# Graph attention, then self-attention: second batch's self_feat as seven half products, gathered additions one a slot, background work moved

## The chip, the cores and the metric

The kernel runs on one core of a Trainium2 chip. The metric is device time in microseconds (us) for one execution. A core has several engines, each working through its own queue in order: TensorE (PE; matmuls and transposes), VectorE (DVE), ScalarE (ACT), GpSimd (POOL) and SyncE (SP), which issues DMAs. An engine waits for another's result through semaphores. A queue is strictly in order: an instruction that waits holds up everything behind it on its engine.

## The reference, cut to what matters

Two layers run over x of shape (8, 512, 512), float32. The change touches layer 0 only.

```
def layer0(v, q, adj, ...):                    # B=8, N=512, F=512, 16 heads, 20 neighbours
    row_zero = v.sum(-1) == 0
    q_exp = where(row_zero[..., None], 0, q[:, None, :])
    self_feat = concat([v, q_exp], -1) @ W_self.T + b_self
    output = self_feat
    for d in range(2):
        A = adj or its transpose, [:, :, :20, :]
        cond, vb = A.sum(-1), A @ w_bias + b_bias
        output += gat_attention(self_feat, cond, vb, Wq[d], bq[d], Wk[d], bk[d], Wout[d], bout[d])
    return v + relu(output)

def gat_attention(self_feat, cond, vb, ...):
    kv = self_feat[:, :20]
    aff = (q . k) / sqrt(dh);  aff = where(cond > 0, aff, -9e15) + vb
    w = softmax(aff)                           # over the 20 neighbours
    return (w @ kv) through Wout, per head
```

Layer 1 is a conditional layer norm, a 16-head self-attention with softmax, an output projection, a residual and a second conditional layer norm.

## The kernel before

**Layout.** P = 128 partitions, so a batch of 512 rows is C = 4 row blocks. B = 8 batches times 4 blocks gives 32 *slots* (b, c), numbered n = 4b + c. Layer 0 walks through the slots; layer 1 follows with 16 steps a batch. The instruction order is written out by hand (`manual_schedule`), so the order of the source is the order of each engine's queue.

**One slot of layer 0, as the main loop writes it.** `turn_weights(n)` transposes the finished softmax weights of slot n on PE (`ptw`, L564) and ACT copies them (L566). `normalize0(n+1)`: exponential on ACT (L553), sum `den` (L556) and reciprocal (L557) on DVE, multiplication on POOL (L558). `scores0(n+2)`: 8 matmuls `pss` (L532) on PE, two additions of the query row on DVE (L536), the mask multiplication on POOL (L538). `add_edges(n+2)`: POOL (L542). Then come products for a later batch's self_feat. `result0(n)`: matmuls `po` (L574, L576) on PE, x = relu + x on DVE (L577), a store. `edges` for a later batch (DVE, L258 to L264), between whose halves `less_top(n+2)` stands: maximum `top` on DVE (L549), subtraction on POOL (L550). Then come loads and background work at the end of the slot. So slot n+2's weights pass L536, L538, L542, L549 and L550 in slot n, and L553, L556, L557 and L558 in slot n+1.

A PE matmul of float32 appears in the profile as two rows, so "x8" of L359 is one product of four matmuls, and "x8" of L312 is four matmuls of 512 columns.

**self_feat in seven products.** For batches 2 to 7, W_self and the transposed x are split in quarters, and the eight quarter products are replaced by seven (numbered 1 to 7, in `self_feat_product`, L359), with sums of weight quarters (`weight_sums0`, L338, DVE, once) and of x quarters (`turned_sums`, L345, POOL, four a batch). Products 1, 6 and 7 build up running sums `ys` (L364 on ACT, L369 on DVE) and add to the list TO_ADD0 one, one and two pending additions of such a sum onto a quarter of self_feat. These are the gathered additions (L699, DVE). Products 2 to 5 are added directly (L373). In slots with c = 2 and 3 products (1, 2) and (6, 7) of batch b + 2 are made, in slots with c = 0 and 1 products (4, 5) and (3) of batch b + 1. At the end of each slot, all pending additions run: one after c = 2, three after c = 3. Batches 0 and 1 use the plain form, 16 matmuls of 512 columns (L312) and an addition for each of four blocks (L320).

**Other background work.** `live_sums(b+2)` (ACT, four sums over rows of x, L293, and one small DVE instruction `lt`, L295) stands at the end of slots with c = 0; `live_of(b+2)` (four PE transposes `pl`, L301, ACT copy, L303) before `result0` in slots with c = 1. `far_away(b+1)` (DVE, L269, L270) stands at the end of slots with c = 1. `norm_stats` (DVE L93 to L96, POOL L97) of layer 1's first batch stand at the end of slots 15 to 18, `norm` (L111) at the end of 22 and 23, two each. In slots 24 and 25 `turn` (L124, PE) transposes what `norm` made.

**PSUM.** Single banks come in turn from a pool of four (products, `po`, `pl`, `pw`), pairs of banks from a pool of two (`pss`, `ptw`).

Of the kernel before, what the change touches and what calls it, by code (L numbers as in the profile page):

```python
# [9 lines left out]
F32 = mybir.dt.float32  # L10
# [3 lines left out]
ALU = mybir.AluOpType  # L14
# [4 lines left out]
B, N, F = 8, 512, 512  # L19
P = 128  # L20
# [5 lines left out]
D2 = 2 * NG  # L26
# [18 lines left out]
def graph_then_self_attention(ctx: ExitStack, tc: tile.TileContext, x, x_t, near, near_t, labels, w_self_t, wq, wk_t,  # L45
# [128 lines left out]
    with ExitStack() as l0:  # L174
# [40 lines left out]
        def load_vt(b):  # L215
            VT[b] = turned.tile([P, C, N], F32, tag="turned", name=f"vt_{b}")
            for cut in (slice(0, 2), slice(2, C)) if b == 0 else (slice(0, C),):
                nc.sync.dma_start(VT[b][:, cut], blocks(x_t[b])[:, cut])
# [20 lines left out]
            nc.vector.memset(head[DH * j:DH * (j + 1), j:j + 1], 1.0)  # L239

        MASK, ADD, LABELS = {}, {}, {}

        def load_labels(b, halves=(0, 1)):
            for i in halves:
                LABELS[b, i] = two.tile([P, 2, D2 * L], I32, tag="labels", name=f"labels_{b}_{i}")
                nc.sync.dma_start(LABELS[b, i], labels[b, i * N // 2:(i + 1) * N // 2, :].rearrange("(c p) m -> p c m", p=P))

        def edges(b, c, halves=(0, 1)):


            if c == 0 and 0 in halves:
                MASK[b] = two.tile([P, C, D2], F32, tag="mask", name=f"mask_{b}")
                ADD[b] = two.tile([P, C, D2], F32, tag="add", name=f"add_{b}")
            src = LABELS[b, c // 2][:, c % 2, :].rearrange("p (m l) -> p m l", l=L)
            weighted = src.bitcast(F32)
            total = two.tile([P, D2], F32, tag="total", name=f"total_{b}_{c}_{halves[0]}")
            if 0 in halves:
                nc.vector.tensor_reduce(total, src, AX.X, ALU.add)  # L258
                nc.vector.tensor_scalar(MASK[b][:, c, :], total, 0.0, None, ALU.is_gt)
            if 1 not in halves:  # L260
                return
            nc.vector.tensor_tensor(weighted, src, edge_bc[:, None, 0:L].to_broadcast([P, D2, L]), ALU.mult)
            nc.vector.tensor_reduce(total, weighted, AX.X, ALU.add)
            nc.vector.tensor_scalar(ADD[b][:, c, :], total, edge_bc[:, L:L + 1], None, ALU.add)  # L264

        def far_away(b):

# [29 lines left out]
        def live_of(b):  # L297

            pl = bank(f"pl_{b}") if b else pair("pl_0")[:, 0, :]
            for c in range(C):  # L300
                nc.tensor.transpose(pl[:, c * P:(c + 1) * P], LT[b][:, c:c + 1].to_broadcast([P, P]), ident)  # L301
            LIVE[b] = two.tile([P, N], F32, tag="live", name=f"live_{b}")
            nc.scalar.copy(LIVE[b], pl)  # L303
# [18 lines left out]
        def self_feat(b, blocks_of_f):  # L322

            self_feat_rest(b, self_feat_main(b, blocks_of_f))
# [15 lines left out]
        def turned_sums(b, n):  # L340

            B11, B12, B21, B22 = (quarter(VT[b], p, q) for p in range(2) for q in range(2))
            TB[n] = {0: B12, 3: B21}.get(n) or parts.tile([P, 2, M], F32, tag=f"t{n}", name=f"ts{n + 1}_{b}")
            x0, x1 = ((B12, B11), (B22, TB.get(0)), (B22, B12), (B21, TB.get(1)))[n]
            nc.gpsimd.tensor_tensor(TB[n], x0, x1, ALU.subtract)  # L345

        def self_feat_product(b, n):
# [24 lines left out]
            for p, q in {2: ((0, 0),), 3: ((0, 1),), 4: ((1, 0),), 5: ((1, 1), (0, 1))}.get(n, ()):  # L372
                nc.vector.tensor_tensor(quarter(SF[b], p, q), o, quarter(SF[b], p, q), ALU.add)  # L373

        def q_row(b):
            QR[b] = two.tile([P, HM], F32, tag="q_row", name=f"q_row_{b}")
            nc.sync.dma_start(QR[b], q_d[b].partition_broadcast(P))
# [54 lines left out]
        far_away(0)  # L432
        load_vt(1)
        load_labels(1)

        kt = pro.tile([P, 2, HG, 2 * MH], F32, name="kt")
        made = kv.tile([P, C, HM], F32, tag="kv", name="made").rearrange("p c m -> p (c m)")
# [103 lines left out]
        def add_edges(b, c, engine=nc.gpsimd):  # L541
            engine.tensor_tensor(T[b, c], T[b, c], ADD[b][:, c, None].to_broadcast([P, H, D2]), ALU.add)  # L542
# [26 lines left out]
        def result0(b, c):  # L569
            cut = slice(c * P, (c + 1) * P)  # L570
            po = bank(f"po_{b}_{c}")

            for g in range(HG):
                nc.tensor.matmul(po[:, g * P:(g + 1) * P], SF[b][:, g, cut], ident, is_transpose=True, start=(g == 0), stop=False)  # L574
            for i in range(KB):
                nc.tensor.matmul(po[:, 96 * i:96 * i + P], WT[b, c][:, i, :], vo[:, b % 2, i, :], start=False, stop=(i == KB - 1))  # L576
            nc.vector.scalar_tensor_tensor(X[b][:, c, :], po, 0.0, X[b][:, c, :], ALU.max, ALU.add)  # L577
            nc.sync.dma_start(mid[b, c * P:(c + 1) * P, :], X[b][:, c, :])
# [42 lines left out]
        for c in (0, 1):  # L621
            edges(1, c)
        live_of(1)
        self_feat(1, (0, 1))
        load_vt(2)
        turned_sums(2, 2)
        for n, (b, c) in enumerate(slots):
            turn_weights(b, c)

            if n + 3 == len(slots):  # L630
                scores0(*slots[n + 2])
            if n + 1 < len(slots):
                normalize0(*slots[n + 1])
            if n + 3 < len(slots):
                scores0(*slots[n + 2])
            if n + 2 < len(slots):
                add_edges(*slots[n + 2], nc.vector if n + 3 == len(slots) else nc.gpsimd)
            if n < 2:
                self_feat(1, (c + 2,))
            elif b + 1 + c // 2 < B:  # L640
                for i in ((4, 5), (3,), (1, 2), (6, 7))[c]:
                    self_feat_product(b + 1 + c // 2, i)
            if 26 <= n < len(slots) - 2:
                less_top(*slots[n + 2])
            if c == 1 and b + 2 < B:
                live_of(b + 2)
                if b + 3 < B:
                    load_vt(b + 3)
            if n in (10, 11, 12, 13):
                keys(1, n - 10, 0)  # L650
            if n in (24, 25):
                for f in (2 * (n - 24), 2 * (n - 24) + 1):
                    turn(0, f)
            group = {26: lambda: q_or_k(0, 0), 27: lambda: q_or_k(1, 0), 29: lambda: value(0), 30: lambda: value(1),
                     31: lambda: value(2)}.get(n, lambda: None)()
            if group:
                group.half(0)
                if n < 30:
                    group.half(1)
            if n == 10:  # L660
                gate_columns(gb)
            result0(b, c)
            if n >= 30:
                group.half(1)
            if b + 1 + c // 2 < B:
                edges(b + 1 + c // 2, (c + 2) % 4, (0,))
            if n < 26:
                less_top(*slots[n + 2])
            if n in (10, 11, 12, 13):
                keys(1, n - 10, 1)  # L670
            if b + 1 + c // 2 < B:
                edges(b + 1 + c // 2, (c + 2) % 4, (1,))
            if c == 0 and b + 2 < B:
                live_sums(b + 2)
            if c == 1:
                if b + 1 < B:
                    far_away(b + 1)
                    load_vo(b + 1)
                if b + 2 < B:
                    load_labels(b + 2, (1,))  # L680
            if c == 0 and b + 2 < B:
                load_labels(b + 2, (0,))
            if c == 2 and b + 2 < B:
                q_row(b + 2)
            if c == C - 1 and b + 3 < B:
                load_x(b + 3)
            if n == 4:
                WG = [weight("wg", wg_t), weight("wb", wb_t)]
            if n == 8:
                gb = gate_vectors()  # L690
                WQ.update({(d, 1): weight(f"wq{d}_1", wq[d]) for d in range(2)})

            if n < 2:
                for i in ((0, 1), (3, 2))[n]:
                    weight_sums0(i)
            if b + 2 + c // 3 < B:
                turned_sums(b + 2 + c // 3, (0, 1, 3, 2)[c])
            for sf, y in TO_ADD0:
                nc.vector.tensor_tensor(sf, y, sf, ALU.add)  # L699
            TO_ADD0.clear()  # L700

            if n in (17, 18, 19, 24):
                i = min(n - 17, 3)
                W1.append(weight(f"w1_{i}", (*(wqkv_t[i] for i in range(3)), wp_t)[i]))
            if n in (23, 28):
                fetch((n - 23) // 5)
            if n == 9:
                early = weight("early", mid[0])
            if 15 <= n < 19:
                norm_stats(0, n - 15, early)  # L710
            for i in {22: (0, 1), 23: (2, 3)}.get(n, ()):
                norm(0, i, early)


# [493 lines left out]
```

## Time and profile before

| | us |
|---|---|
| three runs | 1315.42, 1317.75, 1318.74 (median 1317.75) |
| the profiled execution: time / span | 1315.49 / 1313.7 |
| layer 0's prologue, until slot 0 starts | 76.60 |
| layer 1, from the end of slot 31 to the end of the span | some 913 |

The granted TensorE clock is 1.00 in every window. A slot's start is the start of its first L564 transpose in TensorE's timeline:

| slot | start | slot | start | slot | start |
|---|---|---|---|---|---|
| 0 | 76.60 | 6 | 135.67 | 20 | 287.71 |
| 1 | 86.44 | 15 | 237.46 | 21 | 298.69 |
| 2 | 96.72 | 16 | 247.32 | 22 | 307.75 |
| 3 | 106.58 | 17 | 257.84 | 23 | 317.66 |
| 4 | 116.44 | 18 | 267.12 | 24 | 328.08 |
| 5 | 126.60 | 19 | 277.79 | 25 | 340.54 |

How to read the profile's lines: a line of the timeline gives start, duration, engine, source line, operation, output <- inputs, shapes, count, and in brackets the idle time before it with what ended it. A line of waits gives who waited for whom, total us, times, and the longest. `ts` and `vt` are the x quarters and their sums, `sf` is self_feat, `t` are the scores of a slot.

### The profile page before, as it was taken

The numbers are of one execution on the slowest core, as the hardware profiler recorded it, in microseconds if no ns is written. First come the engines' busy times: TensorE is split into PE (matmuls) and PEld (weight loads), VectorE is DVE, ScalarE is ACT, GpSimd is POOL, SyncE is SP. The second block draws the span as 40 slices with busy tenths as digits, with TensorE's granted clock in tenths as the row PEclk, the third lists the DMA queues.
The fourth block names the chain that finished last, engine by engine and source line by source line (L and its number), as shares of the span: only waits on it lengthen the run. The fifth ranks groups of instructions, "written<-read, shape, count | busy, mean of one in ns | idle before, by whom it ended". The sixth has DMA issues, their size and how long they took to land.

```text
span 1313.7 us, 29713 instructions
## 1 busy us (share of the span) xinstructions
PE 1295.4 (99%) x11347; PEld 988.2 (75%) x11347; DVE 974.7 (74%) x1775; ACT 710.1 (54%) x1740; POOL 842.1 (64%) x905
## 2 busy tenths in 40 slices
PE   9999999999999999999999999999999999999997
PEld 6568887777765687777777777777777777777775
DVE  4479887888746678587677859767775976776886
ACT  2333233223225566766666676675666666666664
POOL 0067775677653546677578667747856775775776
PEclk9999999999999999999999999999999999999999
DMA  9533553253221000001002000100200010010010
GB/s 344 180 108 115 179 194 104 96 180 95 92 80 57 1 1 2 2 17 66 1 1 81 1 2 17 66 2 2 81 2 1 18 66 1 2 50 1 10 42 33
DMA packets 46491, 78.65 MB, mean 60 GB/s; under 512 B 9680, under 2 KB 14224, under 8 KB 46352
## 3 DMA queue, kind: packets, MB, share of 16 engines
q1 hardware_dynamic: 45920, 76.22, 17.0%
q8 instruction: 91, 1.49, 0.5%
q10 hardware_dynamic: 432, 0.55, 0.1%
q14 instruction: 48, 0.39, 0.1%
HBM read 59.27 MB, written 17.49 MB: 58 GB/s over the span
## 4 chain that ended last, share of the span: by engine, by line
PE 87%; DVE 8%; POOL 2%; issue 1%; ACT 1%; DMA 0%; POOLq 0%; DVEq 0%; ACTq 0%
PE pst L793 19%; PE pt L949 17%; PE s L924 10%; PE pss L532 8%; PE pao L964 8%; PE psp L836 6%; PE psf_p L359 4%; PE psf L312 2%; PE po L576 2%; PE pqk L138 2%; DVE top L931 2%; PE pz L124 1%; PE ptw L564 1%; PE pw L501 1%; PE pq L482 1%
## 5 line engine op out<-in xcount | busy, mean ns | idle before, releaser
L944 POOL TENSOR_SCALAR e<-e,den 128x512 f32<-128x512 f32 x511 | 366.8, 718 | 262.4 <-DVE den L941 168.5
L936 ACT ACTIVATE e<-s,top 128x512 f32<-128x512 f32 x512 | 348.9, 699 | 131.4 <-DVE top L931 131.2
L931 DVE TENSOR_REDUCE top<-s 128x2 f32<-128x1024 f32 x256 | 301.2, 1218 | 18.5 <-PE s L924 17.1
L949 PEld LDWEIGHTS pt<-ident,e 128*128 128x128 f32 x2048 | 234.5, 141 | 82.5 <-POOL e L944 25.9
L949 PE MATMUL pt<-ident,e 128*128 128x128 f32 x2048 | 289.7, 276 | 3.4 <-ACT et L951 1.3
L951 ACT COPY et<-pt 128x512 f32<-128x512 f32 x369 | 209.6, 597 | 101.1 <-PE pt L949 100.5
L924 PE MATMUL s<-k_pair,q_pair 32*128 32x512 f32 x992 | 143.8, 640 | 0.0
L532 PE MATMUL pss<-kq,sf 128*128 128x320 f32 x512 | 142.9, 432 | 0.0
L964 PEld LDWEIGHTS pao<-et,v 128*32 128x32 f32 x4096 | 107.5, 110 | 44.4 <-issue 44.4
L964 PE MATMUL pao<-et,v 128*32 128x128 f32 x4096 | 126.5, 274 | 0.0
L532 PEld LDWEIGHTS pss<-kq,sf 128*128 128x128 f32 x512 | 94.9, 190 | 36.1 <-ACT kq L489 0.3
L936 ACT ACTIVATION_READ_ACCUMULATOR e<-s,top 128x1 f32 x512 | 109.4, 214 | 0.0
L951 DVE COPY et<-pt 128x512 f32<-128x512 f32 x143 | 96.4, 674 | 3.4 <-PE pt L949 2.8
L538 POOL TENSOR_TENSOR t<-t,mask 128x640 f32<-128x640 f32 x32 | 49.5, 1547 | 65.6 <-DVE t L536 65.6
L558 POOL TENSOR_TENSOR t<-t,den 128x640 f32<-128x640 f32 x32 | 40.7, 1273 | 54.9 <-DVE den L557 54.3
L553 ACT ACTIVATE t<-t 128x640 f32<-128x640 f32 x32 | 23.6, 738 | 91.5 <-POOL t L550 91.5
L550 POOL TENSOR_TENSOR t<-t,top 128x640 f32<-128x640 f32 x32 | 47.4, 1480 | 38.9 <-DVE top L549 38.9
L126 ACT ACTIVATE ht<-pz,gates_t 128x512 f32<-128x512 f32 x32 | 24.7, 778 | 64.2 <-PE pz L124 64.2
L924 PEld LDWEIGHTS s<-k_pair,q_pair 32*128 32x128 f32 x992 | 41.2, 182 | 20.8 <-issue 17.4
L566 ACT COPY wt<-ptw 128x640 f32<-128x640 f32 x32 | 22.2, 694 | 61.2 <-PE ptw L564 61.1
L851 DVE TENSOR_TENSOR xq<-psp,xq 128x512 f32<-128x512 f32 x30 | 20.2, 689 | 45.9 <-PE psp L836 40.7
L793 PE MATMUL pst<-t,w 128*128 128x256 f32 x224 | 53.7, 383 | 0.0
(272 smaller groups left out, 2286.4 us busy)
## 6 DMA issues: line engine op xcount, KB each, us to landing
x<-in_x SPq DMA_DIRECT2D x8, 1024.0 KB
mid<-x SPq DMA_DIRECT2D x32, 256.0 KB
xq<-mid SPq DMA_DIRECT2D x8, 1024.0 KB
out<-o SPq DMA_DIRECT2D x31, 256.0 KB
vt<-in_x_t SPq DMA_DIRECT2D x7, 1024.0 KB
labels<-in_labels SPq DMA_DIRECT2D x16, 440.0 KB
wq<-in_wq SPq DMA_DIRECT2D x4, 1024.0 KB
gate<-gates SPq DMA_DIRECT2D x8, 512.0 KB
```

The costliest lines, as they stand in the source:

```text
L359: nc.tensor.matmul(o[:, m, :], a[:, k, m * P:(m + 1) * P], t[:, k, :], start=(k == 0), stop=(k == 1))
L532: nc.tensor.matmul(o, SF[b][:, k, cut], KQ[b][:, k, on], start=(k == 0), stop=(k == C - 1))
L538: nc.gpsimd.tensor_tensor(t, t, MASK[b][:, c, None].to_broadcast([P, H, D2]), ALU.mult)
L793: nc.tensor.matmul(out[:, m, :], fixed[:, k, m * P:(m + 1) * P], moving[:, k, :], start=(k == 0), stop=(k == 1))
L836: nc.tensor.matmul(out[:, m, :], t[:, k, m * P:(m + 1) * P], a[:, k, :], start=(k == 0), stop=(k == 1))
L924: nc.tensor.matmul(S[n][j // 2][:, j % 2, :], Q[b, g][on, c * P:(c + 1) * P], K[b, g][on, :], start=True, stop=True)
L931: nc.vector.tensor_reduce(TOP[n][:, 2 * pair:2 * pair + 2], S[n][pair], AX.X, ALU.max, negate=True)
L936: nc.scalar.activation(e, S[n][pair][:, j % 2, :], AF.Exp, bias=TOP[n][:, j:j + 1], accum_out=DEN[n][:, j:j + 1])
L944: engine.tensor_scalar(E[n][j], E[n][j], DEN[n][:, j:j + 1], att_scale, ALU.mult, ALU.mult)
L949: nc.tensor.transpose(pt[:, k * P:(k + 1) * P], E[n][j][:, k * P:(k + 1) * P], ident)
L951: copy(et, pt.rearrange("p (k n) -> p k n", k=C))
L964: nc.tensor.matmul(PAO[b, g][DH * j:DH * (j + 1), at], V[b][:, k, DH * h:DH * (h + 1)], ET[n, j][:, k, :], start=(k == 0), stop=(k == C - 1))
```

## The change

- Batch 1's self_feat uses the seven products. The weight sums and three of its x quarter sums move into the prologue, before the key projections; the fourth stands after product 2. Products 1, 2, 6 and 7 and all gathered additions they leave stand before slot 0, products 5 and 3 in slot 0, product 4 in slot 1. `turned_sums(2, 2)` moves from before slot 0 to its end.
- At the end of each slot one pending gathered addition runs, instead of all.
- `live_sums` moves from the end of slots with c = 0 into those with c = 1, before the product; `live_of` there moves behind `result0`.
- The mask and the last step of the bias in `edges` become `tensor_tensor` with a broadcast column (a zero tile, and the bias column) instead of `tensor_scalar`.
- `norm_stats` in slots 15 to 18 move ahead of `less_top`; `norm` of blocks 0 and 1 go to the ends of slots 21 and 22.

New lines of the changed kernel that the prediction names: L261 is the mask (before: L259).

```diff
+        nothing = pro.tile([P, 1], F32, name="nothing")
+        nc.vector.memset(nothing, 0.0)
...
-                nc.vector.tensor_scalar(MASK[b][:, c, :], total, 0.0, None, ALU.is_gt)
+                nc.vector.tensor_tensor(MASK[b][:, c, :], total, nothing.to_broadcast([P, D2]), ALU.is_gt)
...
-            nc.vector.tensor_scalar(ADD[b][:, c, :], total, edge_bc[:, L:L + 1], None, ALU.add)
+            nc.vector.tensor_tensor(ADD[b][:, c, :], total, edge_bc[:, L:L + 1].to_broadcast([P, D2]), ALU.add)
...
+        def add_gathered0(some=None):
+            for sf, y in TO_ADD0[:some]:
+                nc.vector.tensor_tensor(sf, y, sf, ALU.add)
+            del TO_ADD0[:some]
...
         load_labels(1)
+        for i in (0, 1, 3, 2):
+            weight_sums0(i)
+        for i in (2, 0, 1):
+            turned_sums(1, i)
...
         live_of(1)
-        self_feat(1, (0, 1))
+        for i in (1, 2, 6, 7):
+            self_feat_product(1, i)
+            if i == 2:
+                turned_sums(1, 3)
+                add_gathered0()
         load_vt(2)
-        turned_sums(2, 2)
+        add_gathered0()
...
+            if c == 1 and b + 2 < B:
+                live_sums(b + 2)
             if n < 2:
-                self_feat(1, (c + 2,))
+                for i in ((5, 3), (4,))[n]:
+                    self_feat_product(1, i)
             elif b + 1 + c // 2 < B:
...
-            if c == 1 and b + 2 < B:
-                live_of(b + 2)
-                if b + 3 < B:
-                    load_vt(b + 3)
+            if c == 1 and b + 3 < B:
+                load_vt(b + 3)
...
             result0(b, c)
+            if c == 1 and b + 2 < B:
+                live_of(b + 2)
...
                 edges(b + 1 + c // 2, (c + 2) % 4, (0,))
+            if 15 <= n < 19:
+                norm_stats(0, n - 15, early)
             if n < 26:
                 less_top(*slots[n + 2])
...
-            if c == 0 and b + 2 < B:
-                live_sums(b + 2)
...
-            if n < 2:
-                for i in ((0, 1), (3, 2))[n]:
-                    weight_sums0(i)
+            if n == 0:
+                turned_sums(2, 2)
...
-            for sf, y in TO_ADD0:
-                nc.vector.tensor_tensor(sf, y, sf, ALU.add)
-            TO_ADD0.clear()
+            add_gathered0(1)
...
-            if 15 <= n < 19:
-                norm_stats(0, n - 15, early)
-            for i in {22: (0, 1), 23: (2, 3)}.get(n, ()):
+            for i in {21: (0,), 22: (1,), 23: (2, 3)}.get(n, ()):
                 norm(0, i, early)
```

## The prediction

> **What bounds the kernel now.** I read the page first, then who waited for whom on TensorE in layer 0, then the timeline of each engine around one of those waits.
>
> ```profile
> PE 1295.4 (99%) x11347; PEld 988.2 (75%) x11347; DVE 974.7 (74%) x1775; ACT 710.1 (54%) x1740; POOL 842.1 (64%) x905
> ```
>
> TensorE is busy nearly throughout, so only two things are worth time: fewer matmuls, and its few stops. In layer 0, from 60 to 420 us, these are:
>
> ```profile
> PE ptw L564 <- POOL t L558: 3.5, 7, 1.0
> PE pq L482 <- DVE x L577: 1.6, 4, 0.4
> PE po L574 <- DVE sf L373: 1.4, 1, 1.4
> ```
>
> These waits understate the stops, because each restart also loses some overlap. I use slot lengths instead: a slot runs from the first `ptw` of its turn to the next slot's. Without a stop TensorE needs 9.86 us (0.55 ptw, 4.31 pss, two products at 1.725, 0.43 + 1.12 po, as in slot 15), and 8.57 us in slots with c = 1 (one product and 0.43 for `pl`). By the table of starts, slots 4 and 5 take 0.8 us too much together, and slots 16 to 24 take 6.2 (340.54 - 247.32 = 93.22, against 87.02, slot 24 needing 10.72 with its `turn`). That is 7.0 us of stops.
>
> Slot 20 shows the cause, on VectorE, GpSimd and ScalarE in turn:
>
> ```profile
> 290.71 0.82 DVE L549 TENSOR_REDUCE top<-t 128x32 f32<-128x640 f32 x1
> ...
> 292.73 0.49 DVE L264 TENSOR_SCALAR add<-total,vec 128x40 f32<-128x40 f32 x1
> 293.14 2.96 DVE L699 TENSOR_TENSOR sf<-ys,sf 128x512 f32<-128x512 f32 x3
> 296.02 0.81 DVE L556 TENSOR_REDUCE den<-t 128x32 f32<-128x640 f32 x1
> ...
> 299.66 0.68 DVE L577 SCALAR_TENSOR_TENSOR x<-po,x 128x512 f32<-128x512 f32 x1
> ```
>
> ```profile
> 291.61 1.58 POOL L550 TENSOR_TENSOR t<-t,top 128x640 f32<-128x640 f32 x1 [0.93 <-DVE top L549]
> 293.14 1.80 POOL L345 TENSOR_TENSOR ts<-vt 128x512 f32<-128x512 f32 x1
> 297.36 1.27 POOL L558 TENSOR_TENSOR t<-t,den 128x640 f32<-128x640 f32 x1 [2.41 <-DVE den L557]
> 298.59 1.55 POOL L538 TENSOR_TENSOR t<-t,mask 128x640 f32<-128x640 f32 x1
> ```
>
> ```profile
> 293.21 0.74 ACT L553 ACTIVATE t<-t 128x640 f32<-128x640 f32 x1 [4.01 <-POOL t L550]
> 296.42 0.63 ACT L293 ACTIVATE x<-x 128x512 f32<-128x512 f32 x1 [2.47 <-DMA x<-in_x]
> ```
>
> The exponential ends at 293.95, but `den` starts at 296.02: three gathered additions stand before it. The next slot's `ptw` follows `den` by 2.67 us (298.69).
>
> **The rule of a slot.** From such rows: `den` can start 3.27 us after `top`; L262 to L264 fill 2.43 of that, so 0.84 us of background is free and the rest delays `den`. The next slot starts at the later of TensorE's own work and den + 2.67. The next `top` comes at den + 2.57 + 3.19 (L538, L542) or at x + 1.35, where x is the next slot's start + 0.2, or den + 3.65 for c = 0.
>
> **Part 1, products.** Sixteen 512-column matmuls (3.43 us per four, 13.73) become 28 of 256 columns (seven at 1.725, 12.08): -1.65 us.
>
> **Part 2, what the products put in front of slot 1.** Ahead of `den` stood two sf additions; now stand seven of 0.60 us (one sf, two ys, four gathered):
>
> ```profile
> 82.20 0.81 DVE L556 TENSOR_REDUCE den<-t 128x32 f32<-128x640 f32 x1
> ```
>
> `den` goes to 85.2, so slot 1 starts at 87.87 instead of 86.44. Then `top` is at 85.2 + 5.76 = 90.96, L550 ends at 93.45, and GpSimd now has two turned sums behind it instead of one:
>
> ```profile
> 90.42 1.29 POOL L345 TENSOR_TENSOR vt<-vt 128x512 f32<-128x512 f32 x1
> 94.24 1.27 POOL L558 TENSOR_TENSOR t<-t,den 128x640 f32<-128x640 f32 x1 [2.54 <-DVE den L557]
> ```
>
> They end at 96.0, L558 at 97.25. With part 4 slot 2 starts at 97.4 (before: 96.72), so the 1.65 us are lost again for the moment. Between all adds hidden and a second wait of a turned sum (1.29), this is 0 to 3.8 us; I take 2.4.
>
> The weight sums (four at 0.60) go into VectorE's idle 2.37 us before 38.09; TensorE has 0.36 us of slack there (the last key copy ends at 39.68, the next pq starts at 40.04), so 0; without that cover 2.4. GpSimd idles until 66.22, which hides three turned sums; if their input landed just within 35.7 to 38.1, sums on both engines would take turns and cost up to 3.9. SP issues that load from 28.9 to 32.7, behind other megabytes, so I take 0. No SP entry changes its place. In c = 1 slots the transposes `pl` and their bank come after `po`; in slot 13 their copy is waited for in place of x, below 0.3 us either way.
>
> **Part 3, gathered additions one a slot.** After c = 3 two of three leave, one with a lock wait (2.88 to 0.60): `den` 2.0 us earlier. One each arrives after c = 0 (free, 0.60 < 0.84) and c = 1. There `far` and L270 already take 1.47, so 0.60 is added to `den`, before a 9.86 us slot that has 0.8 to spare.
>
> **Part 4, live sums behind the exponential of c = 1.** Four sums take 2.57 us (124.89 to 127.46), `lt` and its semaphores about 0.2, `pl` 0.43: the next slot can't start before den + 3.2 instead of den + 2.67. Behind `lt` on VectorE wait the product's addition, x and the mask; x moves to den + 3.3, before the next `top` needs it. TensorE reaches `pl` 8.14 us into the slot, so this costs something only if the exponential ends later than 5.4 us into it. The gain is that ScalarE no longer waits 2.47 us for the load of x; nothing was queued there that ended a slot.
>
> **Part 5, mask and add as tensor_tensor.** The L259 rows last 0.18 to 1.54 us, the long ones until a GpSimd instruction ends. Does the new form wait too?
>
> ```profile
> 272.92 1.28 DVE L270 TENSOR_TENSOR add<-add,far 128x160 f32<-128x160 f32 x1
> ...
> 272.66 1.36 POOL L345 TENSOR_TENSOR ts<-vt 128x512 f32<-128x512 f32 x1
> ```
>
> L270 is a tensor_tensor of two SBUF operands; it takes 0.33 us in the idle prologue and 1.28 beside GpSimd. L262, with a broadcast operand, goes from 0.60 to 0.985. So I take the waits as unchanged (0). The other end is the free 0.18 at each L259. The rows don't show an operand of one column. The Trainium skill (SBUF — State Buffer, "Who interferes with whom") says that a VectorE instruction with two SBUF inputs contends with a GpSimd instruction that reads SBUF, whatever their shapes; by it the swap gives nothing, by the free rows it gives rival A's sum.
>
> **Part 6, statistics ahead of `top`, norms spread.** With a mask that waits until L542 ends, 1.0 us of statistics delays `top` in slots 15 to 17, but no longer `den`; GpSimd's pow (0.55) hides under `top` (0.82). Norms: one in 21, one in 22 instead of two.
>
> **The sum.** By the rule, slots start so (before in brackets): 6 at 135.55 (135.67): the gathered additions are gone from slots 3 and 4, and the lost start is made good. From 247.32, leaving this 0.12 out: 17 at 257.18 (257.84); 18 at 266.4 (267.12), held by `pl`; 19 at 277.13 (277.79), with `den` at 274.46 behind far and one addition; 20 at 286.99 (287.71); 21 at 296.85 (298.69); 22 at 305.42 (307.75); 23 at 315.28 (317.66); 24 at 325.14 (328.08). There `den` is at 331.45, the first L373 ends 2.53 later at 333.98, and TensorE reaches po at 334.3, so the 1.4 us stop goes: 25 at 335.86 (340.54), -4.68. Together -4.8 us. Layer 1 starts earlier by that, and the busy times by window give TensorE 399.74 of the 400 us from 500 to 900, so it arrives at the end. The profiled execution took 1315.49 us (span 1313.7 and 1.8 outside): 1310.7. It lies 2.26 under the median of 1317.75, on which the forecast stands: 1313.0.
>
> **Rivals.** A: the new form doesn't wait, and every stop goes: -1.65 - 0.8 - 6.2 = -8.6, 1309.1. For it: L262's operand is eleven columns wide, L270's 160, and no row has one of a single column. Against: both wait. Chance 0.18. B: an addition that is now alone loses the port to L345, as one in three does now (L699: 1.75 us, against 0.68). Its 1.67 us then delay `den` by 0.83 in most slots; half of the 4.7 and the 0.9 of slots 4 and 5 go: -1.5, 1316.2. Against: the first one after L264 has won each time. Chance 0.17. C, slower: the live sums. If exponentials end 6.4 us into the c = 1 slots, as in 5, 17 and 21 now, the next start is 6.4 + 2.77 + 0.43 = 9.6 after the slot's, 1.03 late, in six slots (6.2), with part 2's 2.4, less 1.65 and a further 2.0 from part 3: +5, 1322.7. It decides from 5.4 us on; part 3 pulls the exponentials below that. Chance 0.10.
>
> **How the numbers follow.** The forecast has 0.55. About 0.3% (4.0 us) is what a measurement of this kernel can tell from no change. The forecast passes 1313.8 by only 0.8, so two thirds of it count as faster (0.37); with A 0.55. The rest with B is within 0.3% (0.35); C is slower (0.10). The range reaches from A, 1308.8, to above B, 1317.0, which leaves out C and the tails.
>
> **What would show it.** Slot 2 starting 0.7 later than now; slots 21 to 25 without waits on L558 and no wait of po on L373; one L699 row a slot, at 0.68; L261 still reaching 1.5 us; `pl` in slot 17 waiting for `lt`. I am wrong if L261 stays at 0.2, or if `pl` waits in most c = 1 slots.

## The result, and the profile after

The changed kernel takes 1322.18 us (median of 10 runs, 1320.28 to 1322.5), the kernel before, run beside it, 1317.42 (10 runs, 1315.12 to 1318.74): a ratio of 1.0039, with an interval of 1.003 to 1.0048. It is slower by 4.8 us; 1313.0 was predicted, in a range that ended at 1317.0. The profiled execution took 1320.40 us, span 1318.6.

Slot starts (us) show where. They are counted from each execution's own slot 0, which starts between 76.2 and 79.0 us from one execution to the next:

| slot | before | forecast | after | after, with only L266 as before (`e1_scalar_add`) | best (`h3_start_cleared`) |
|---|---|---|---|---|---|
| 1 | 9.84 | 11.27 | 12.38 | 12.45 | 9.86 |
| 2 | 20.12 | 20.8 | 22.69 | 22.77 | 18.44 |
| 6 | 59.07 | 58.95 | 62.16 | 60.92 | 56.59 |
| 17 | 181.24 | 180.6 | 184.97 | 182.01 | 177.68 |
| 18 | 190.52 | 189.8 | 196.02 | 191.24 | 186.53 |
| 20 | 211.11 | 210.4 | 216.81 | 211.79 | 206.25 |
| 22 | 231.15 | 228.8 | 237.29 | 230.22 | 224.68 |
| 25 | 263.94 | 259.1 | 269.30 | 261.35 | 255.80 |

(The forecast is that of the prediction, less before's slot 0 at 76.60, with its 0.12 us of slot 6 taken along at slot 25.) The changed kernel lies 5.4 us behind the kernel before at slot 25, and 10.2 behind the forecast. Of these 10.2, 1.9 are there at slot 2; the rest grows from slot to slot.

The first part of the page of the changed kernel, busy time by engine:

```profile
PE 1295.6 (98%) x11371; PEld 993.2 (75%) x11371; DVE 993.1 (75%) x1783; ACT 710.1 (54%) x1741; POOL 841.6 (64%) x909
```

VectorE is busy 18 us longer for eight instructions more, while GpSimd's time is unchanged. Who waited for whom on TensorE, from 60 to 430 us (total, times, longest):

```profile
PE pl L303 <- DVE lt L297: 5.6, 4, 2.3
PE ptw L575 <- POOL t L569: 3.8, 4, 2.3
...
PE po L585 <- DVE sf L375: 0.3, 1, 0.3
```

The stop of po shrank as forecast; the `ptw` waits stand at 3.8 us, and a new wait of 5.6 us, for `lt`, is the largest. Slot 20 on VectorE and then on GpSimd, in the changed kernel:

```profile
296.43 0.82 DVE L560 TENSOR_REDUCE top<-t 128x32 f32<-128x640 f32 x1
...
298.45 0.51 DVE L266 TENSOR_TENSOR add<-total,vec 128x40 f32<-128x40 f32 x1
298.88 1.80 DVE L379 TENSOR_TENSOR sf<-ys,sf 128x512 f32<-128x512 f32 x1
300.61 0.81 DVE L567 TENSOR_REDUCE den<-t 128x32 f32<-128x640 f32 x1
```

```profile
297.33 1.58 POOL L561 TENSOR_TENSOR t<-t,top 128x640 f32<-128x640 f32 x1 [0.93 <-DVE top L560]
298.87 1.27 POOL L347 TENSOR_TENSOR ts<-vt 128x512 f32<-128x512 f32 x1
```

One gathered addition stands there instead of three, as intended, but it lasts 1.80 us instead of 0.68: it starts 0.01 us behind GpSimd's turned sum and first waits for the 1.27 us of that. `den` starts 4.18 us after `top`, not 3.27, and the next slot at 303.27, which is den + 2.66: the rule of a slot holds, its input is wrong. All gathered additions of the changed kernel, as one group:

```profile
L379 DVE TENSOR_TENSOR sf<-ys,sf 128x512 f32<-128x512 f32 x28 | 32.4, 1164 | 0.0
```

At 0.68 each they would be busy 19 us; twelve last 1.80.

### The profile page after: what moved, and what is told of

Its sections match the earlier page's. It is cut to its first block, busy times and chain, and to the rows that moved or that the text cites. A ratio compares the mean times of both kernels' runs of the same rounds, so it can differ in the third digit from the quotient of the medians.

```text
span 1318.6 us, 29770 instructions
## 1 busy us (share of the span) xinstructions
PE 1295.6 (98%) x11371; PEld 993.2 (75%) x11371; DVE 993.1 (75%) x1783; ACT 710.1 (54%) x1741; POOL 841.6 (64%) x909
## 4 chain that ended last, share of the span: by engine, by line
PE 79%; DVE 15%; POOL 2%; issue 2%; ACT 1%; DMA 0%; POOLq 0%; DVEq 0%; ACTq 0%
PE pst L806 19%; PE pt L962 17%; PE s L937 10%; PE pao L977 8%; PE psp L849 6%; PE pss L543 5%; PE psf_p L361 2%; PE pqk L138 2%; DVE sf L379 2%; DVE top L944 2%; PE po L587 1%; PE pz L124 1%; PE pw L512 1%; DVE mask L261 1%; PE pq L493 1%
## 5 line engine op out<-in xcount | busy, mean ns | idle before, releaser
L561 POOL TENSOR_TENSOR t<-t,top 128x640 f32<-128x640 f32 x32 | 47.4, 1481 | 36.4 <-DVE top L560 36.4
L937 PEld LDWEIGHTS s<-k_pair,q_pair 32*128 32x128 f32 x992 | 41.2, 182 | 20.8 <-issue 17.4
```

The costliest lines, as they stand in the source:

```text
L561: nc.gpsimd.tensor_tensor(tv, tv, top.to_broadcast([P, 2 * H, NG]), ALU.subtract)
L937: nc.tensor.matmul(S[n][j // 2][:, j % 2, :], Q[b, g][on, c * P:(c + 1) * P], K[b, g][on, :], start=True, stop=True)
```

## The experiments

The theory after this look: VectorE's gathered addition and GpSimd's turned sum take turns (the prediction says that one of them wins or loses the port). The new form of the bias step (L266) decides which of the two goes first, and every addition that loses delays `den`, then the exponential, then `lt`. Its rivals: the moved sums are themselves the cause; the new start is; or the lost turn comes from something else. Each single run below has runs of the kernel before beside it.

### The form of one 0.2 us instruction

`e1_scalar_add`, and the same kernel timed as `f4_scalar_add_timed`, undo in the changed kernel:

```diff
-            nc.vector.tensor_tensor(ADD[b][:, c, :], total, edge_bc[:, L:L + 1].to_broadcast([P, D2]), ALU.add)
+            nc.vector.tensor_scalar(ADD[b][:, c, :], total, edge_bc[:, L:L + 1], None, ALU.add)
```

> The changed kernel with only the bias column's addition (L266) back as tensor_scalar. Theory: as tensor_tensor it ends a few hundredths of a us later, so GpSimd's turned sum (L347) takes the port first and the single gathered addition behind it lasts 1.80 us. Then here the additions after c = 0, 2 and 3 last 0.68 us again, L347 lasts 1.80, den comes 1.1 us earlier, and slot 25 starts at 342.5 to 343.8 instead of 345.81 (span about 1316). Rival: an addition that stands alone loses the port whatever stands before it. Then the rows stay at 1.80 us and slot 25 stays within 0.4 of 345.8.

> The changed kernel with only L266 back as tensor_scalar, timed in five rounds. Theory: the profiled 8.4 us below the changed kernel are no accident of one execution: 3 to 5 us below the kernel before, ratio 0.996 to 0.998. Rival: the race for the port falls differently from run to run: times spread over 3 us and more, ratio 0.998 to 1.002.

Measured: 1311.95 us (before 1315.78); timed, a median of 1312.47 against 1316.56, ratio 0.997 (0.9959 to 0.9981). Slot 25 comes 7.95 us earlier than in the changed kernel, over twice what was expected of the theory. The same slot 20, VectorE and GpSimd:

```profile
292.50 0.49 DVE L266 TENSOR_SCALAR add<-total,vec 128x40 f32<-128x40 f32 x1
292.91 0.68 DVE L379 TENSOR_TENSOR sf<-ys,sf 128x512 f32<-128x512 f32 x1
293.75 0.82 DVE L567 TENSOR_REDUCE den<-t 128x32 f32<-128x640 f32 x1 [0.17 <-ACT t L564]
```

```profile
291.38 1.57 POOL L561 TENSOR_TENSOR t<-t,top 128x640 f32<-128x640 f32 x1 [0.93 <-DVE top L560]
292.92 1.80 POOL L347 TENSOR_TENSOR ts<-vt 128x512 f32<-128x512 f32 x1
```

In both kernels L266 starts 1.12 us after L561 and L347 1.54 us after it. The addition starts 0.43 us after L266 as tensor_tensor, 0.41 as tensor_scalar. So it comes 0.01 us behind L347 or 0.01 ahead of it, and whoever is behind takes 1.8 us. Here it is GpSimd, which has the time. The group of additions:

```profile
L379 DVE TENSOR_TENSOR sf<-ys,sf 128x512 f32<-128x512 f32 x28 | 18.9, 680 | 0.0
```

The expectation was too small, most likely because a late `den` is passed on: it makes the exponential late, and in slots with c = 1 the sums behind it, `lt` and `pl`. The waits for `lt` fall from 5.6 us to 0.5 without any change to the sums.

`g1_before_column_add` makes the same edit the other way round in the kernel before (L264 there becomes tensor_tensor, nothing else):

> The kernel before with only L264 as tensor_tensor of a broadcast column. Theory: GpSimd's turned sum then takes the port first, so the first gathered addition after c = 2 and 3 lasts 1.80 us, but the second after c = 3 no longer waits (1.75 to 0.68): only c = 2 is later, by 1.1 us, and slot 25 starts 0 to 2 us later than 340.54. Rival: the form costs the 8 us of the changed kernel by itself: slot 25 at 345 or later.

Measured: 1324.40 us (before 1315.57), slot 25 later by 7.66, not by the 0 to 2 expected: the rival was right. Its waits on TensorE:

```profile
PE ptw L564 <- POOL t L558: 8.8, 11, 1.3
```

In the kernel before they were 3.5 us in seven. The form alone costs the old kernel as much as the new one, so neither the one addition a slot nor the moved sums is needed for it.

`g2_scalar_mask_only` undoes the mask's form (L261) and keeps that of the bias step:

> The changed kernel with only the mask (L261) back as tensor_scalar. Theory: both forms of the mask wait for the port alike, so slot 25 stays within 0.6 of 345.81 and the gathered additions at 1.80. Rival: the mask's form has a part in it, and slot 25 moves by 1.0 or more.

Measured: 1322.07 us, slot 25 at 268.97 against 269.30; twelve additions last 1.80 as before. The mask's form has no part in the 8 us.

### Order in time, or the form of the instruction?

`h1_short_op_between` keeps tensor_scalar (as e1) and puts an instruction of 0.06 us that uses no SBUF input ahead of the addition; `h2_turned_sum_later` keeps the changed kernel's tensor_tensor and puts one of 0.09 us ahead of GpSimd's turned sum.

```diff
 (h1, beside L266 as in e1; both allocate `spare`)
...
+            nc.vector.memset(spare, 0.0)
             add_gathered0(1)
...
 (h2)
             if b + 2 + c // 3 < B:
+                nc.gpsimd.memset(spare, 0.0)
                 turned_sums(b + 2 + c // 3, (0, 1, 3, 2)[c])
```

> The changed kernel with the scalar addition (L266), and one short VectorE instruction (a memset of one column, some 0.1 us) ahead of the gathered addition of each slot. Theory: the order in time decides, by a few hundredths of a us: GpSimd's turned sum goes first, the additions after c = 0, 2 and 3 last 1.8 us again, and slot 25 starts 268 to 271 us after slot 0 (269.30 in the changed kernel, 261.35 with the scalar addition alone). Rival: the scalar form keeps GpSimd out in some other way: the additions stay at 0.68, slot 25 at 262 or less after slot 0.

> The changed kernel with the tensor_tensor kept (L266), and one short GpSimd instruction (a memset of one column, some 0.1 us) ahead of each slot's turned sum. Theory: the order in time decides, so the gathered addition goes first: 0.68 us, turned sums 1.80, slot 25 at 261 to 263 after slot 0 (269.30 in the changed kernel). Rival: after a tensor_tensor of two SBUF operands GpSimd goes first whatever the order: 1.80 us rows stay and slot 25 stays at 268 or more.

Measured: h2 takes 1312.54 us (before 1317.26), slot 25 at 261.07, and every addition lasts 0.68. Its slot 20 on VectorE, then on GpSimd:

```profile
292.85 0.51 DVE L267 TENSOR_TENSOR add<-total,vec 128x40 f32<-128x40 f32 x1
293.28 0.68 DVE L380 TENSOR_TENSOR sf<-ys,sf 128x512 f32<-128x512 f32 x1
```

```profile
293.25 0.09 POOL L715 MEMSET spare<- 128x1 f32 x1
293.31 1.79 POOL L348 TENSOR_TENSOR ts<-vt 128x512 f32<-128x512 f32 x1
```

Here 0.09 us on GpSimd give back the 8 us. h1 takes 1319.53 us, slot 25 at 266.86, slightly less late than expected: the short instruction moves the addition's start by about 0.01 us only, and nine of twelve are lost. One of the nine, with the turned sum below it:

```profile
298.15 0.49 DVE L267 TENSOR_SCALAR add<-total,vec 128x40 f32<-128x40 f32 x1
298.57 1.81 DVE L380 TENSOR_TENSOR sf<-ys,sf 128x512 f32<-128x512 f32 x1
298.58 0.06 DVE L716 MEMSET spare<- 128x1 f32 x1
298.56 1.27 POOL L348 TENSOR_TENSOR ts<-vt 128x512 f32<-128x512 f32 x1
```

So the additions are lost with tensor_scalar too, and won with tensor_tensor in h2: the order in time decides, not the form of L266. (The memset stands ahead of the addition in the queue, yet is recorded 0.02 us behind it: recorded starts this close can't be taken as exact.)

All runs say the same, where a lone addition and a turned sum start within 0.03 us of each other. The addition's start less the sum's, from the timelines of the two engines:

| L266 as | kernels | addition's start less the sum's | additions of 1.8 us |
|---|---|---|---|
| tensor_tensor | after, e2, e3, e5, g1, g2 | +0.01 to +0.02 | 62 of 62 |
| tensor_scalar | before, e1, f1 to f4, g3, g4, h3, h4 | -0.01 to 0.00 | 0 of 104 |
| tensor_scalar, short instruction behind it | h1 | 0.00 to +0.01 | 9 of 12 |
| tensor_tensor, short instruction on GpSimd | h2 | -0.03 to -0.02 | 0 of 12 |

Two groups of rows stand outside this table. In f1, f2 and f3 (below) `lt` comes between L266 and the addition after c = 0. The addition then starts 0.06 to 0.07 us behind the sum, and all ten such rows last 1.76 or 1.77 us. And before slot 0 another two-input instruction of `edges` (L262 before, L264 after) meets a turned sum: 0.01 to 0.03 us behind it, it lost in all eleven kernels that show this; with starts equal to within 0.01 us it won in the kernel before and lost in f1, f2, g1 and g2. So which of two equal starts wins can't be read off the starts.

### The live sums

`e2_sums_back` puts `live_sums` and `live_of` back to their old places in the changed kernel; `f3_add_and_sums` does so in e1.

```diff
-            if c == 1 and b + 2 < B:
-                live_sums(b + 2)
...
+            if c == 1 and b + 2 < B:
+                live_of(b + 2)
...
             result0(b, c)
-            if c == 1 and b + 2 < B:
-                live_of(b + 2)
...
+            if c == 0 and b + 2 < B:
+                live_sums(b + 2)
```

> The changed kernel with live_sums and live_of back in their old places, all else kept. Theory: the waits of pl for lt (5.6 us in slots 5, 9, 17 and 21) are a cost of their own: slot 6 starts 0.8 earlier, slot 10 0.6, and slot 25 at about 343.0 (span about 1315.8). Rival: they stand in for waits of ptw on L569 that come anyway, since the den of those slots is as late: then slot 25 moves by less than 1.0 and the waits on L569 grow by what pl loses.

> The changed kernel with the scalar addition (L266) and with live_sums and live_of in their old places. Theory: with the port won the exponentials come early enough and the moved sums cost little: within 1.0 us of the kernel with the scalar addition alone (slot 25 at 337.0 to 338.3). Rival: the moved sums cost 3 us or more even then: slot 25 at 335 or earlier.

Measured: e2 1320.08 us, slot 25 at 268.99. The waits for `lt` fall from 5.6 to 1.3 us, and this takes their place:

```profile
PE ptw L575 <- POOL t L569: 7.5, 10, 2.3
```

So the stops named after `lt` were those of a late `den` under another name. f3 takes 1313.26 us, ratio 0.9976 (0.9967 to 0.9985), slot 25 at 262.64, 1.3 us later than e1. Once the additions win their turn, the move of the sums costs nothing. It may gain a little, though the two intervals overlap: at the old place `lt` makes three additions of f3 lose.

### The start

`e3_plain_batch1` takes batch 1 back to its sixteen plain matmuls, with the old prologue:

```diff
-        for i in (0, 1, 3, 2):
-            weight_sums0(i)
-        for i in (2, 0, 1):
-            turned_sums(1, i)
...
-        for i in (1, 2, 6, 7):
-            self_feat_product(1, i)
...
+        self_feat(1, (0, 1))
...
-                for i in ((5, 3), (4,))[n]:
-                    self_feat_product(1, i)
+                self_feat(1, (c + 2,))
...
```

> The changed kernel with batch 1 back on the 16 plain matmuls, the weight sums back in slots 0 and 1 and turned_sums(2, 2) back before slot 0. Theory: the start alone costs 2.5 us that nothing later makes good: slot 2 starts at 96.7 instead of 99.20, no half clock in slot 1, and slot 25 at 343.3 (span 1316.1). Rival: the later slots wait for the same chain whatever the start, and slot 25 stays within 0.5 of 345.8.

Measured: 1320.13 us; slot 2 at 20.27, as in the kernel before, but slot 25 at 268.25. So the start is where the first 2.4 us are lost. Only 1.05 of them are still there at slot 25; that the later slots' own lost turns hide the rest fits this, but isn't shown apart.

In the changed kernel TensorE stops for 2.35 us before slot 1, and what follows is slow:

```profile
88.89 0.77 PE L575 MATMUL ptw<-ident,t 128*128 128x128 f32 x5 [2.35 <-POOL t L569]
89.49 6.16 PE L543 MATMUL pss<-kq,sf 128*128 128x320 f32 x16
```

The same matmuls take 4.47 in e2. In the stretch behind the stop (length, busy time of PE, PEld, DVE, ACT and POOL, granted clock, DMA share, GB/s) the clock is halved in the changed kernel, and not in e2 after the same stop:

```profile
90.10:93.50 3.40, 3.40 (x8) 2.21 (x7) 3.33 (x7) 0.29 (x1) 2.39 (x3) 0.50 0.54 170
```

```profile
90.20:93.60 3.40, 3.40 (x14) 2.44 (x13) 3.33 (x7) 0.33 (x1) 2.39 (x3) 1.00 0.52 148
```

`e5_filled_wait` fills the stop with two spare matmuls into a bank that nobody reads:

```diff
         for n, (b, c) in enumerate(slots):
+            if n == 1:
+                spare = bank("spare")
+                for i in range(2):
+                    nc.tensor.matmul(spare, ident, VT[1][:, 0, :], start=True, stop=True)
             turn_weights(b, c)
```

> The changed kernel with two more 512-column matmuls (1.72 us, into a bank that nobody reads) before slot 1's ptw, where TensorE waits 2.35 us. Theory: the half granted clock from 90.1 to 93.5 us follows from that wait; with it filled to 0.6 us the clock stays at 1.00, slot 1 takes 8.55 instead of 10.32 us and slot 2 starts 1.8 earlier (97.4). Rival: the half clock comes from the work itself (pss beside loads and VectorE), and slot 1 stays at 10.3 with a clock of 0.5 for 3.4 us.

Measured: 1320.32 us. The clock stays at 1.00 in slot 1, yet slot 2 comes only 0.3 us earlier counted from slot 0 (22.39 against 22.69; 1.8 were expected), as `pl` then waits 1.22 us for `lt`. So slot 1 is 1.7 us longer at the halved clock (10.31 us, against 8.57 for such a slot without a stop), but most of that lies beside the wait for `lt` that comes up without it. As e2 and h2 keep the full clock behind the same unfilled stop, e5 alone doesn't show that the filling kept it.

Two kernels, both with e1's L266, make `den` of slot 1 earlier instead. `g4_add_and_late` leaves three of batch 1's gathered additions to the ends of slots 0 (two) and 1, and puts `turned_sums(2, 2)` back before slot 0; `h4_edges_early` moves two `edges` that stood before slot 0 (the rows at 75 to 82 us) into the key projections, where VectorE has time.

```diff
 (g4)
         load_vt(2)
-        add_gathered0()
+        turned_sums(2, 2)
...
-            add_gathered0(1)
+            add_gathered0(2 if n == 0 else 1)
 (h4; the first two lines stand in the loop over the key projections)
+            if 3 <= n < 7:
+                edges(1, (n - 3) // 2, ((n - 3) % 2,))
...
-        for c in (0, 1):
-            edges(1, c)
```

> The changed kernel with the scalar addition (L266), turned_sums(2, 2) back before slot 0 and three of batch 1's gathered additions left to slots 0 and 1. Theory: the start's loss is the work in front of den: slot 1 starts at 86.2 to 86.7 (there 88.89), TensorE waits less than 0.5 us, no half clock in slot 1, slot 2 at 95.4 to 96.6 (there 99.21), and slot 25 1.5 to 3.5 earlier than 337.79. Rival: the mask's wait in the prologue or lt holds slot 2 anyway: slot 2 at 97.5 or later.

> The changed kernel with the scalar addition (L266) and only the edges of batch 1's first two blocks moved into the key phase. Theory: they are what makes den late before slot 1 (5.6 us on VectorE with two lock waits): slot 1 starts within 0.5 us of TensorE's own 9.84 us after slot 0 (12.45 with the scalar addition alone), no half clock in slot 1; slot 2 is then held by lt and two turned sums, at 19.0 to 20.3 after slot 0 (22.77). Rival: the seven additions alone make den late: slot 1 at 11 us or more after slot 0.

Measured: g4 1313.07 us, slot 1 at 10.90 but slot 2 at 21.96 (`lt` again holds `pl`, by 2.25 us), slot 25 at 260.57. h4 1309.53 us (before 1317.26): slot 1 at 9.86, slot 2 at 18.43, no halved clock, slot 25 at 257.03, 4.3 us ahead of e1. So the products' additions were late at the start because two `edges`, with two waits for GpSimd, stood ahead of them. In the changed kernel:

```profile
75.98 1.11 DVE L261 TENSOR_TENSOR mask<-total,nothing 128x40 f32<-128x40 f32 x1
77.01 1.72 DVE L264 TENSOR_TENSOR labels<-labels,vec 128x440 f32<-128x440 int32 x1
...
86.22 0.81 DVE L567 TENSOR_REDUCE den<-t 128x32 f32<-128x640 f32 x1
```

### The statistics, the one-a-slot additions alone, and two attempts at the best

`g3_add_and_stats` is e1 with `norm_stats` back at the ends of slots 15 to 18:

```diff
-            if 15 <= n < 19:
-                norm_stats(0, n - 15, early)
             if n < 26:
                 less_top(*slots[n + 2])
...
+            if 15 <= n < 19:
+                norm_stats(0, n - 15, early)
```

> The changed kernel with the scalar addition (L266) and with the statistics of slots 15 to 18 back at the ends of the slots. Theory: ahead of top they delay it by up to 1.0 us in slots 15 to 17, behind it by a part of that, so slots 18 to 20 start 0.3 to 1.0 earlier than with the scalar addition alone (slot 20 at 287.2 to 287.9, there 288.23). Rival: with a gathered addition already there the statistics delay den by as much: slot 20 within 0.3 of 288.23 or later.

Measured: 1314.72 us; slot 20 at 211.49 against 211.79, slot 25 at 261.69 against 261.35. It doesn't tell the two apart: the place of the statistics is worth some 0.3 us, and these two numbers differ in sign.

`f2_one_a_slot` is the kernel before with one gathered addition a slot and the spread norms, and nothing else of the change:

```diff
-            for sf, y in TO_ADD0:
-                nc.vector.tensor_tensor(sf, y, sf, ALU.add)
-            TO_ADD0.clear()
+            add_gathered0(1)
...
-            for i in {22: (0, 1), 23: (2, 3)}.get(n, ()):
+            for i in {21: (0,), 22: (1,), 23: (2, 3)}.get(n, ()):
```

> The kernel before with only two parts of the change: one gathered addition a slot, and the norms spread. Theory: by the rule of a slot, with the port won, slots 4 and 5 lose their 0.8 and slot 25 starts at 335.1 (334 to 336.5); 5 us below the kernel before. Rival: the added addition after c = 1 and lost ports eat it: slot 25 at 338 or later.

Measured: 1313.88 us, ratio 0.9978 (0.997 to 0.9987), slot 25 at 262.21: 1.73 us earlier than before, far from the 5.4 expected. The slots whose `den` stands behind `far` and one addition take 10.58 and 11.26 us (slots 2 and 18), and three additions after c = 0 are lost because `lt` stands ahead of them (1.77 us).

`f1_best` joined e1 with the old mask, the old places of the sums, g4's start and the statistics ahead of `result0`:

```diff
-        add_gathered0()
+        turned_sums(2, 2)
...
+            if 15 <= n < 19:
+                norm_stats(0, n - 15, early)
             result0(b, c)
```

> The changed kernel with both columns back as tensor_scalar, live_sums and live_of in their old places, turned_sums(2, 2) back before slot 0, three of batch 1's four gathered additions left to slots 0 and 1 (two and one), and the statistics of slots 15 to 18 behind the products, ahead of result0. Theory (each cost is named: the port, the start, the sums): slot 1 starts at 86.5, slot 2 at 95.2 to 95.8, gathered additions last 0.68, slot 25 starts at 332.5 to 335, and the time is 8 us (6 to 9) below the kernel before. Rival: once these waits are gone the chain of a slot binds anyway, and it comes out no faster than the changed kernel with the scalar addition alone (some 4 us below the kernel before).

Measured: 1312.51 us, ratio 0.9969 (0.9957 to 0.9982), slot 25 at 261.30: no better than e1, though 8 us below the kernel before were expected. With the sums back, `lt` (0.16 us) stands between L266 and the addition after c = 0, and the additions behind it are lost again, at the ends of slots 0, 4, 16 and 20. That of slot 4:

```profile
132.05 0.49 DVE L266 TENSOR_SCALAR add<-total,vec 128x40 f32<-128x40 f32 x1
132.46 0.16 DVE L297 TENSOR_SCALAR lt<-sums 128x4 f32<-128x4 f32 x1
132.53 1.77 DVE L379 TENSOR_TENSOR sf<-ys,sf 128x512 f32<-128x512 f32 x1
```

It is the same race, lost to another small instruction.

`h3_start_cleared` is h4 with batch 2's live sums and transposes at their old place, `turned_sums(2, 2)` before slot 0 and the statistics ahead of `result0`:

```diff
-            if c == 1 and b + 2 < B:
+            if c == 1 and 0 < b and b + 2 < B:
                 live_sums(b + 2)
...
+            if n == 1:
+                live_of(2)
...
             if n == 0:
-                turned_sums(2, 2)
+                live_sums(2)
...
```

> The changed kernel with the scalar addition (L266); the edges of batch 1's first two blocks in the key phase; batch 2's live sums and live_of in their old places; turned_sums(2, 2) back before slot 0; the statistics of slots 15 to 18 ahead of result0. Theory: each loss is then cleared: slot 2 starts 18.4 to 19.2 us after slot 0, no half clock, slot 25 at 256 to 258 (263.94 before), 6 to 8 us below the kernel before. Rival: the edges delay the key copies (0.36 us of slack each) and the chain of a slot binds at the start as it is: slot 25 at 260 or more, no better than the scalar addition alone.

Measured: 1307.79 us (five runs, 1307.07 to 1309.3) against 1317.26, ratio 0.9934 (0.992 to 0.9948). It beats both kernels. The waits of TensorE from 60 to 420 us, all of them:

```profile
PE pq L493 <- DVE x L588: 1.2, 3, 0.4
PE pt L965 <- ACT et L967: 0.4, 1, 0.4
PE po L585 <- DVE sf L375: 0.2, 1, 0.2
```

No `ptw` and no `pl` waits any more, and the clock stays at 1.00 in slot 1.

## Why the prediction was wrong, point by point

- **Part 5 failed.** "So I take the waits as unchanged (0)": the waits did stay (mask rows still reach 1.43 us, L266 0.51 against 0.49), but what was costed, the instruction's own duration, was the wrong quantity. A start 0.02 us later behind L266 changed which engine goes next. That costs 7.95 us of the 10.2 missed (e1; g1 shows the same 7.66 in the old kernel; h2 takes it back without touching the form). The bounds set for it, from nothing to a gain, did not hold a loss.
- **With it fell the 0.60 us that Part 3 gives to a lone addition.** Part 3 calls it free after c = 0; twelve took 1.80 us. This is what rival B says. The evidence against B was that "the first one after L264 has won each time". That was true of the rows, all of them of the old form, and by a margin of 0.00 to 0.01 us that the rows showed and that I did not weigh. B put the time at 1316.2, 1.5 us below the kernel before, and it came 4.8 above; but it is B's mechanism that came.
- **Part 4 was right, with its condition.** `pl` waits for `lt` if the exponential ends later than 5.4 us into the slot. With `den` late it does. ScalarE in slot 17 (261.48 to 272.53) of the changed kernel:

```profile
267.62 0.74 ACT L564 ACTIVATE t<-t 128x640 f32<-128x640 f32 x1 [4.65 <-POOL t L561]
...
270.62 0.19 ACT L295 ACTIVATION_READ_ACCUMULATOR x<-x 128x1 f32 x1
```

  And on TensorE:

```profile
272.07 0.62 PE L303 MATMUL pl<-ident,lt 128*128 128x128 f32 x4 [2.30 <-DVE lt L297]
```

  The exponential ends 6.9 us into it, the sums end at 270.8, and `pl` stops for 2.30 us. So rival C's size (1322.7) came, though not from C's cause alone: e2, without the moved sums, is as slow.
- **Part 2 was too small by 1.9 us at slot 2.** `den` was forecast at 85.2 and came at 86.22: the seven additions took 4.53 us instead of 4.2, and a wait of L264 was not in the sum: it took 1.72 us, where L262 in the kernel before had taken 0.60. A turned sum stood beside both; in the kernel before it was the sum that lost the turn, in the changed kernel L264. VectorE and GpSimd in the kernel before, then in the changed one:

```profile
77.12 0.60 DVE L262 TENSOR_TENSOR labels<-labels,vec 128x440 f32<-128x440 int32 x1
77.12 1.74 POOL L345 TENSOR_TENSOR ts<-vt 128x512 f32<-128x512 f32 x1
```

```profile
77.01 1.72 DVE L264 TENSOR_TENSOR labels<-labels,vec 128x440 f32<-128x440 int32 x1
76.99 1.27 POOL L347 TENSOR_TENSOR vt<-vt,ts 128x512 f32<-128x512 f32 x1
```

  So it is the same race, left out of the sum a second time. Then slot 1 ran at half clock. A remedy was in reach: h4 shows the additions hidden when the edges go elsewhere.
- **The rule held, and Part 1; Part 3 only together with the rest.** From slot 2 to 25, e1 needs 238.6 us, the forecast 238.3, the kernel before 243.8. Part 1's 1.65 us lie ahead of slot 2: h4, where no stop hides them, reaches slot 2 1.69 us before the kernel before does. Part 3 nearly alone (f2) brings slot 25 forward by 1.73 us of 5.4: three additions lose their turn to `lt` there, but f3, which loses the same three, is only 1.3 us behind e1, so most of f2's shortfall stays open. Part 6 isn't told apart (g3). With that one instruction's form undone, e1 and f4 arrive at 1311.95 and 1312.47 us, beside kernels before at 1315.78 and 1316.56: f4 gains 4.1 us, the forecast was 4.8.
- **Two slips in the sums** change nothing in this: rival A's time stands as 1309.1 and as 1308.8, and the loss of slots 4 and 5 as 0.8 and as 0.9.
- **What the prediction asked to see:** slot 2 came 2.6 us later than before, not 0.7; twelve of 28 L379 rows lasted 1.80; L261 stayed long, and `pl` in slot 17 waited, both as said.

## What to carry to other kernels

Where two engines wait for the same thing to be released, look in the timeline by how much the favoured one is ahead before calling its win a rule; a margin of 0.01 us is no margin, and any edit of the small instruction ahead of it can turn it. Price such a loss by what is passed on (here an addition 1.1 us longer, twelve times, and every slot behind it), and set the order deliberately: a short instruction ahead of the engine that has time to spare gave back 8 us here. A wait that appears under a new name may be the old delay, so undo the suspected cause and the named one separately.

## What the runs showed of the hardware

- **A start 0.02 us earlier or later decides the turn.** In the runs the engine that starts second is held until the other ends, so that the same addition takes 0.68 or 1.80 us and the same turned sum 1.27 or 1.80. The Trainium skill (SBUF — State Buffer, "Who interferes with whom") states that a VectorE instruction with two SBUF inputs contends with GpSimd's reads, and that "Issue order, not op shape, decides who blocks." The table of 190 pairs agrees; the rows of L262 and L264 with equal starts show that a hundredth of a us is too near to call. As h1 and h2 show, the form of L266 mattered by moving the next start by 0.02 us.
- **A stop of about 2.3 us can be followed by 3.4 us at half clock.** The granted clock was 0.50 from 90.1 to 93.5 us after the stop of 2.35 us in the changed kernel, and dropped after the same stop (2.33 to 2.44 us) in e1, f3, f4, g2, g3 and h1 too; in e2 and h2 (2.35 us each) it stayed at 1.00, and in g4 after one of 2.25. After the stop in slot 17 (2.21 to 2.30 us) it dropped in e5 and h1 and not in the changed kernel, e3 and g2. What decides isn't shown, but from 60 to 430 us no run shows a drop without such a stop. The Trainium skill (TensorE: Matmul & The Clock Gate, "Why this matters for your kernels") warns of gaps above about 3 us; here the drops came after shorter ones, in some executions.
